# Score masks in 32-row matmuls, and a liquid state divided by DT * DT

## The chip, the cores and the metric

The kernel runs on one core of a Trainium2 chip. The metric is the time of one execution in device microseconds. The median of eight runs of the kernel before is 1016.46 us, the lowest 1014.69 us, the highest 1020.36 us. Engines are named as in the profile: PE is the tensor engine's matmul, PEld its weight load, DVE the vector engine, ACT the scalar engine, POOL the general-purpose engine, SP the engine that issues the DMAs. PSUM is the memory that matmuls write, in 8 banks of 128 partitions x 512 f32.

## The reference

One decoder block over x of 2 x 1024 tokens x 256 features. What matters here, in short:

```python
# self-attention on LN(LN(x)), 2*2 blocks of 512 tokens, 16 heads of 16; causal
scores = q @ k.T / sqrt(16);  scores[key > query] = -inf
attn = softmax(scores) @ v @ out_w + out_b
# liquid cell, 8 steps, DT = 0.1; ctx = attn, xs starts as LN(x + attn)*g1 + b1, vs as 0
u  = tanh(ctx @ w_ctx + xs @ w_x + b_inl)
vs = vs + DT * (u - xs - vs)
xs = xs + DT * vs
# then: x + xs, LN, GELU feed-forward of 1024, cross-attention to 77 context tokens (16 heads),
# and 8 soft trees of 255 nodes: (x @ W_in.T), silu, one path a tree kept, @ W_out.T
```

The kernel holds the 2 x 1024 tokens as four blocks of 512 (`NTB`), two to a sequence; the queries of a sequence's second block also attend to its first block, whole and without a mask.

## The kernel before, in words

All work is issued by `Clock.weave` (L354). Several threads of stages, written as Python generators, run beside each other: attention scores of blocks 0 and 2, of blocks 1 and 3, weights, the middle (liquid cell, feed-forward, cross-attention) and the trees. A stage yields what it needs next (tiles, banks, or a ready operation), and `weave` takes the one that its own costs say can start first. These costs are written into `Clock`: a change of the PE array's shape (`TURNS`, L100), a matmul, an eviction. So one changed cost moves the order of everything behind it. The order is fixed when the program is built; on the chip each engine works its queue in that order and waits on semaphores.

PE works in three shapes. FULL is 128 rows x 128 columns. ROWS is four groups of 32 rows x 128 columns that work beside each other: a group holds 4 heads, 32 partitions each, and each head is one group of rows. COLUMNS is four groups of 128 x 32, for the products of weights and values.

Causal attention is worked in sets of heads (`Heads`, L71). There are two kinds. `maxima` (L797) writes the scores of one tile of queries with q as the weights and keys as columns, and DVE reads each bank for the maximum. `weighted` (L874) writes transposed scores, and ACT reads each bank for the exponential; POOL clears what lies above the diagonal. A unit has four heads, one PSUM bank each, and `Clock.issue` (L310) writes either all four heads of one unit, or two heads of one and two of a unit of the other engine ("mixed"), or two alone. `Clock.choices` (L278) picks: the price of a mixed pair holds half of the difference of the two spans.

In the block on the diagonal, `maxima` has three units for each of 4 groups and 4 blocks: queries' tiles 0 and 2 together (128 and 384 keys in one bank), tile 1 (256 keys) and tile 3 (512 keys). Their last 128 keys need the causal mask. `masks` (L815) adds it ahead of the scores, one bf16 matmul of the 128 x 128 identity with the 128 x 128 mask for every head and tile, in shape FULL; the scores then follow in shape ROWS onto the same banks. `issue` writes the masks of all heads first (L315-317), then the scores step by step.

`liquid` (L965) keeps two banks of pre-activations for a block. Each of 8 steps takes ACT's tanh into `w`, one DVE add of `r` (or a subtraction of `xs` in the first step), eight matmul instructions with `w_dx` (which is `w_x` times DT * DT, made in `fill_late`, L561), and then on DVE for each half `xs = w * DT*DT + xs` and `r = w * (1 - DT) - xs`. The product ahead of the first step uses `w_x` itself. In the end `add_tokens_first` (L637) transposes `xs` and adds it to `h0` with `add_half` (L652).

`fill` (L548) prepares memory at the start: it clears tiles, and copies mask and identity to bf16.

Of the kernel before, what the change touches and what calls it, by code (L numbers as in the profile page):

```python
# [16 lines left out]
P = 128  # L17
# [53 lines left out]
class Heads:  # L71
# [4 lines left out]

    def __init__(self, banks, columns, one, read, engine, mask=None):
        self.banks, self.one, self.read, self.engine = banks, one, read, engine
        self.mask, self.steps = mask, len(columns)
        self.mode = FULL if mask else ROWS  # L80
        self.span = sum(max(n, P) for n in columns) / 600
        self.left = [0, 2] if engine == "dve" else [2, 0]
        self.over = 0
# [8 lines left out]
class Clock:  # L92
# [185 lines left out]
    def choices(self, t, todo):  # L278
# [15 lines left out]
        one = max(self.pe, ready, free[1][0]) + self.ALONE  # L294
        found.append((one, self.turn(own.mode), [(own, own.left[0])]))
        if len(own.left) == 2:
            found.append((two, self.turn(own.mode), [(own, 0), (own, 2)]))
        for u in todo:
            other = None if isinstance(u["need"], (Op, list)) else u["need"][1]
            if not isinstance(other, Heads) or other.engine == own.engine:  # L300
                continue
            at = max(two, self.ready(u["need"][0]) + self.HANDOVER)
            for j0 in own.left:
                if 2 - j0 in other.left:
                    worth = self.turn(max(own.mode, other.mode)) - self.MIXED
                    worth += abs(own.span - other.span) / 2
                    found.append((at, worth, [(own, j0), (other, 2 - j0)]))
        return found

    def issue(self, heads):  # L310


        heads = [(unit, j0 + i) for unit, j0 in heads for i in range(2)]
        heads = [(unit, j, *unit.banks(1)) for unit, j in heads]
        for unit, j, ps in heads:  # L315
            if unit.mask:
                unit.mask(j, ps)
        self.each = max(unit.span for unit, _, _ in heads) / sum(unit.steps for unit, _, _ in heads)
        for step in range(max(unit.steps for unit, _, _ in heads)):

            for unit, j, ps in reversed(heads):
                if step < unit.steps:
                    unit.one(j, ps, step)
        pairs = []
        for (unit, j0, one), (_, j1, two) in zip(heads[::2], heads[1::2]):
            unit.left.remove(j0)
            pairs.append((unit, self.reading(unit, (unit.read(j0, one), one), (unit.read(j1, two), two))))
        return pairs
# [86 lines left out]
def decoder_kernel(ctx: ExitStack, tc: tile.TileContext, ins: dict, out: bass.AP):  # L415
# [80 lines left out]
    wo = load("wo", (DC, D))  # L496
    w_x = load("w_x", (DC, D))
    xwq = load("xwq", (DC, D))
# [13 lines left out]
    make_causal_mask(nc, mask32, NEG)  # L512
    mask, ident16 = (const.tile([P, P], BF16, tag=n, name=n) for n in ("mask", "ident16"))
    half = const.tile([P, NQ], F32, tag="half", name="half")
# [3 lines left out]
    paths = const.tile([P, 2, P], BF16, tag="paths16", name="paths16")  # L518
    w_dx = const.tile([P, DC, D], F32, tag="w_dx", name="w_dx")
    half_b = const.tile([P, 2 * PAR], F32, tag="half_b", name="half_b")  # L520

# [26 lines left out]
    def fill():  # L548
# [4 lines left out]
        )  # L553
        yield clock.vector("tensor_copy", mask, mask32)
        yield clock.vector("tensor_copy", ident16, ident)
        for t in (v, *xv):
# [4 lines left out]
    def fill_late():  # L561
        for t in (qT[1], xq, *nmax[2:]):
            yield zeros(t)
        yield clock.vector("tensor_copy", paths, paths32)
        yield clock.activation(w_dx, w_x, AF.Copy, scale=DT * DT)
        for name in ("ff", "trees"):
            for w in streams[name]:
# [43 lines left out]
    def scaled(dst, src, mv, rstd):  # L611

        for i in range(NQ):
# [3 lines left out]
            )  # L617

    def evicted(ops, *banks):
        yield ops  # L620
        clock.free(*banks)

    def features_first(dst, src, name, g=None, b=None):

        made = []
        for c in range(DC):
            yield (src,), 1
            ps = bank()
            for i in range(NQ):
                clock.transpose(  # L630
                    ps[:, i * P : (i + 1) * P], src[:, i, c * P : (c + 1) * P], ident
                )
            affine = () if g is None else (col(g, c), col(b, c))
            made.append(clock.beside(evicted(clock.evict(dst[:, c, :], ps, *affine), ps)))
        yield (), lambda: all(m() for m in made)

    def add_tokens_first(dst, src, name):  # L637

        made = []
        for j in range(2):  # L640
            yield (src,), 1
            ps = bank()
            for i in range(2):
                for c in range(DC):
# [3 lines left out]
                    )  # L648
            made.append(clock.beside(add_half(dst, j, ps)))
        yield (), lambda: all(m() for m in made)  # L650

    def add_half(dst, j, ps):  # L652

        at = dst[:, 2 * j : 2 * j + 2, :]
        yield clock.vector("tensor_tensor", at, at, ps.rearrange("p (i d) -> p i d", d=D), ALU.add)
        clock.free(ps)
# [98 lines left out]
    def norms(tb, x):  # L755
# [6 lines left out]
        xn = atile(f"xn{tb}", "xn", 2)  # L762
        yield from features_first(xn, xc, f"attn{tb}", "g_attn", "b_attn")
        return xn
# [32 lines left out]
    def maxima(tb, g, qT):  # L797
# [14 lines left out]
        for parts in units:  # L812
            diagonal = parts[0][1] == blk

            def masks(j, ps):  # L815
                for _, _, n, at in parts:
                    clock.matmul(
                        ps[:, at + n - P : at + n], ident16, mask, start=at == 0, stop=False,
                        skip_group_check=True,
                    )  # L820

# [20 lines left out]
            k = parts[0][1] * TB  # L842
            heads = Heads(banks, columns, one, read, "dve", masks if diagonal else None)
            yield (qT[:, g, :], kT[:, g, k : k + TB]), heads
# [100 lines left out]

    def layernorm(src, name, g=None, b=None, known=None):

# [4 lines left out]
        dst = dtile(f"xn_{name}")  # L952
        yield from features_first(dst, xc, name, g, b)
        return dst
# [10 lines left out]
    def liquid(tb, h0, aT):  # L965
# [8 lines left out]
        done.add((tb, "o"))  # L974
        xs = yield from layernorm(h0, f"l1_{tb}", "g1", "b1", block[tb]["known"])
        yield from add_product(ps, w_x, xs)
        r = dtile(f"r{tb}")
        for it in range(NITER):


# [3 lines left out]
            for c in range(DC):  # L984
                if it == 0:
                    yield clock.vector("tensor_tensor", w[:, c, :], w[:, c, :], xs[:, c, :], ALU.subtract)
                else:
                    yield clock.vector("tensor_tensor", w[:, c, :], w[:, c, :], r[:, c, :], ALU.add)
            if it < NITER - 1:
                yield from add_product(ps, w_dx, w)  # L990
            for c in range(DC):
                yield clock.vector("scalar_tensor_tensor", 
                    xs[:, c, :], w[:, c, :], DT * DT, xs[:, c, :], ALU.mult, ALU.add
                )
                if it < NITER - 1:
                    yield clock.vector("scalar_tensor_tensor", 
                        r[:, c, :], w[:, c, :], 1.0 - DT, xs[:, c, :], ALU.mult, ALU.subtract
                    )
        clock.free(*ps)
        yield from add_tokens_first(h0, xs, f"xs{tb}")  # L1000

# [11 lines left out]
    def feed_forward(tb, x, h0):  # L1013
        hn = yield from layernorm(h0, f"l2_{tb}", "g2", "b2")
        yield clock.vector("tensor_tensor", x, x, h0, ALU.add)
# [390 lines left out]
```

## Time and profile before

| what | value |
| --- | --- |
| median of 8 runs | 1016.46 us |
| profiled execution | 1016.75 us, its span 1015.0 us, so 1.7 us lie around the span |
| granted PE clock over the span | 0.988 |
| POOL, DMA | busy 82.2 us; 44.87 MB moved, mean 44 GB/s |
| masks | 256 matmuls of 128 x 128 bf16 |
| scores, DVE's kind / ACT's kind | 768 / 768 matmul passes |
| liquid cell | 224 matmul passes, 184 large DVE operations |

A record of a matmul lasts longer than the array is taken: it runs from its issue to the write of its last result. An f32 matmul is two passes, and each is a record. "Busy" of a group is the union of its records. A timeline line merges records of one kind that follow each other: its first number is the start, its second the time from that start to the last record's end.

### The profile page before, as it was taken

The page shows a single profiled execution, that of the slowest core. Times are in us where ns is not written, and L with a number is a line of the kernel's source. Part 1 is how long each engine was busy: PE and PEld are TensorE (multiplying, and loading weights), DVE is VectorE, ACT ScalarE, POOL GpSimd, SP SyncE. Part 2 cuts the span into 40 slices and gives each one's busy share as a digit, 9 for nine tenths or more (in the row PEclk, how much of TensorE's full clock was granted, in tenths as well). Part 3 has the DMA queues.
Part 4 walks back from the last instruction along what each step waited for, and adds up shares of the span by engine and source line. Part 5 has one row for each costly group of instructions (what it writes and reads, how often), then busy time and mean ns, then how long its engine had stood idle before and what let it go on. Part 6 is the DMA issues. An engine that isn't in the chain of part 4 may idle for free.

```text
span 1015.0 us, 14070 instructions
## 1 busy us (share of the span) xinstructions
PE 964.7 (95%) x5496; PEld 486.0 (48%) x5496; DVE 620.9 (61%) x1345; ACT 412.5 (41%) x695; POOL 82.2 (8%) x161
## 2 busy tenths in 40 slices
PE   6899899899999999999999999999999999999898
PEld 4544444345446445564444433346455446645443
DVE  4757768953544798608766996841465881555444
ACT  4153344533473234415444444542643423353331
POOL 0111101010101002102100101010100000000000
PEclk9799999999999999999999999999999999999999
DMA  8220001002000001123000001102200021101211
GB/s 286 63 46 19 1 1 42 1 21 84 22 2 21 32 10 44 31 73 94 22 11 12 12 21 42 43 13 88 67 12 32 31 84 52 44 30 58 83 63 57
DMA packets 22338, 44.87 MB, mean 44 GB/s; under 512 B 2944, under 2 KB 3328, under 8 KB 22272
## 3 DMA queue, kind: packets, MB, share of 16 engines
q1 hardware_dynamic: 22272, 43.97, 13.8%
q8 instruction: 43, 0.70, 0.3%
q14 instruction: 23, 0.19, 0.1%
HBM read 35.57 MB, written 2.10 MB: 37 GB/s over the span
## 4 chain that ended last, share of the span: by engine, by line
PE 87%; DVE 7%; ACT 4%; DMA 1%; issue 1%; SPq 0%; ACTq 0%; DVEq 0%
PE bank L165 81%; PE bank L181 6%; ACT p L197 2%; DVE nmax L207 2%; DVE top L207 2%; DVE ta L207 1%; DMA xwk_sb<-in_xwk_dram 1%; ACT xp L197 0%; ACT th L197 0%; DMA xn<-in_xtok_dram 0%; DVE xn_l L207 0%; DVE x L207 0%; ACT ta L197 0%; DVE r L207 0%; DVE xc_l L207 0%
## 5 line engine op out<-in xcount | busy, mean ns | idle before, releaser
L197 ACT ACTIVATE p<-bank 128x512 f32<-128x512 f32 (+1 forms) x320 | 155.4, 556 | 153.3 <-PE bank L165 143.6
L207 DVE TENSOR_REDUCE top<-bank 128x1 f32<-128x512 f32 (+3 forms) x256 | 138.1, 583 | 47.1 <-PE bank L165 46.8
L165 PE MATMUL bank<-qT,kT 32*128 32x512 f32 (+3 forms) x768 | 131.4, 534 | 7.8 <-ACT p L197 3.4
L165 PE MATMUL bank<-kT,qT 32*128 32x512 f32 (+3 forms) x768 | 131.9, 543 | 6.8 <-ACT p L197 4.0
L165 PE MATMUL bank<-ta,trees 128*128 128x512 f32 x256 | 126.2, 601 | 2.7 <-DVE ta L207 2.5
L165 PE MATMUL bank<-xn_t,trees 128*128 128x512 f32 x256 | 126.6, 604 | 0.4 <-ACT p L197 0.2
L207 DVE TENSOR_REDUCE nmax<-bank 128x4 f32<-128x308 f32 (+4 forms) x192 | 83.5, 479 | 39.5 <-PE bank L165 37.0
L165 PE MATMUL bank<-w,w_dx 128*128 128x512 f32 x224 | 102.7, 598 | 1.4 <-DVE w L207 1.4
L207 DVE TENSOR_TENSOR x<-x,bank 128x512 f32<-128x512 f32 x40 | 27.3, 685 | 115.3 <-PE bank L165 115.1
L216 POOL TENSOR_SCALAR_AFFINE_SELECT p<-p 128x256 f32<-128x256 f32 x128 | 56.5, 463 | 400.9 <-ACT p L197 226.4
L197 ACT ACTIVATE th<-bank,half_b 128x512 f32<-128x512 f32 x64 | 44.1, 689 | 100.6 <-PE bank L165 100.6
L197 ACT ACTIVATE w<-bank,b_ac 128x512 f32<-128x512 f32 x64 | 43.9, 688 | 86.9 <-PE bank L165 86.8
L165 PE MATMUL bank<-p,v 128*32 128x512 f32 (+3 forms) x768 | 72.3, 500 | 1.4 <-DVE nmax L207 1.0
L165 PEld LDWEIGHTS bank<-ta,trees 128*128 128x128 f32 x256 | 46.2, 190 | 52.9 <-issue 42.9
L165 PEld LDWEIGHTS bank<-xn_t,trees 128*128 128x128 f32 x256 | 44.7, 190 | 51.6 <-issue 43.0
L165 PEld LDWEIGHTS bank<-qT,kT 32*128 32x128 f32 x768 | 48.1, 188 | 40.6 <-ACT p L197 13.3
L165 PEld LDWEIGHTS bank<-w,w_dx 128*128 128x128 f32 x224 | 41.3, 190 | 53.4 <-issue 41.2
L165 PEld LDWEIGHTS bank<-kT,qT 32*128 32x128 f32 x768 | 43.6, 189 | 48.4 <-ACT p L197 11.6
L165 PE MATMUL bank<-xn_l,ff 128*128 128x512 f32 x128 | 59.7, 594 | 0.0
L165 PE MATMUL bank<-ff,ht 128*128 128x256 f32 x256 | 59.2, 379 | 0.0
L207 DVE SCALAR_TENSOR_TENSOR ta<-ta,th 128x1024 f32<-128x1024 f32 x32 | 39.1, 1222 | 30.2 <-ACT ta L197 30.1
L165 PEld LDWEIGHTS bank<-ff,ht 128*128 128x128 f32 x256 | 48.6, 190 | 16.9 <-issue 11.5
(168 smaller groups left out, 1165.1 us busy)
## 6 DMA issues: line engine op xcount, KB each, us to landing
trees<-in_trees_dram SPq DMA_DIRECT2D x64, 256.0 KB, 2.6
ff<-in_ff_dram SPq DMA_DIRECT2D x32, 256.0 KB, 3.0
xn<-in_xtok_dram SPq DMA_DIRECT2D x4, 512.0 KB, 4.1
qT<-qc SPq DMA_DIRECT2D x16, 128.0 KB, 2.3
kT<-kc SPq DMA_DIRECT2D x16, 128.0 KB, 2.3
kc<-in_xtok_dram SPq DMA_DIRECT2D x4, 512.0 KB, 4.4
x<-in_xtok_dram SPq DMA_DIRECT2D x4, 512.0 KB, 4.0
xq<-xqc SPq DMA_DIRECT2D x16, 128.0 KB, 2.3
```

Source lines behind the costliest of these rows:

```text
L165: return self.nc.tensor.matmul(out, w, x, **kw)
L181: return self.nc.tensor.transpose(out, x, ident)
L197: lambda: self.nc.scalar.activation(out, x, func, bias=bias, scale=scale),
L207: "dve", cost, 0.085, out, args, lambda: getattr(self.nc.vector, name)(out, *args, **kw)
L216: self.nc.gpsimd.affine_select(out=out, in_=args[0], **kw)
```

## The change

- Masks. `mask` and `ident16` become tiles of 4 x 128 columns in which every group of 32 rows holds one 32-row slice after another, so that the four heads' groups of rows can each add the mask by themselves. A mask of one head and tile is now four bf16 matmuls in shape ROWS (32 rows each), over the last 128, 96, 64 and 32 columns, since the first 32 rows of the mask touch all columns and later ones fewer. `issue` runs them as the first steps of a head, interleaved over the heads like the scores. A unit's span counts 0.056 us for each mask step, and no unit asks for shape FULL any more.
- Making those tiles: `fill` copies mask and identity to bf16, spreads the identity over `rows`, and multiplies eight times 128 x 128 on PE into two banks, which are copied out.
- Liquid cell. The state is `z = xs / (DT*DT)`: scale and bias of its LayerNorm are divided by DT * DT into `g1b1` once. The first product uses `w_dx` as the others do. The add after tanh becomes `w = r * DT*DT + w`; `r` is worked out from the old `z`; the state's update becomes the plain sum `z = z + w`, which is issued beside the rest and only has to be done before the next `r`. `add_half` multiplies by DT * DT when it adds the state to `h0`.
- `w_x` is loaded into one of the trees' buffers, since it is used only to make `w_dx`.

```diff
-    def __init__(self, banks, columns, one, read, engine, mask=None):
+    def __init__(self, banks, columns, one, read, engine, mask=None, masks=0):
...
-        self.mode = FULL if mask else ROWS
-        self.span = sum(max(n, P) for n in columns) / 600
+        self.span = sum(max(n, P) for n in columns) / 600 + masks * 0.056
...
-        found.append((one, self.turn(own.mode), [(own, own.left[0])]))
+        found.append((one, self.turn(ROWS), [(own, own.left[0])]))
...
-                    worth = self.turn(max(own.mode, other.mode)) - self.MIXED
+                    worth = self.turn(ROWS) - self.MIXED
                     worth += abs(own.span - other.span) / 2
...
-        for unit, j, ps in heads:
-            if unit.mask:
-                unit.mask(j, ps)
-        self.each = max(unit.span for unit, _, _ in heads) / sum(unit.steps for unit, _, _ in heads)
-        for step in range(max(unit.steps for unit, _, _ in heads)):
+        n = sum(unit.masks + unit.steps for unit, _, _ in heads)
+        self.each = max(unit.span for unit, _, _ in heads) / n
+        for step in range(max(unit.masks + unit.steps for unit, _, _ in heads)):
             for unit, j, ps in reversed(heads):
-                if step < unit.steps:
-                    unit.one(j, ps, step)
+                if step < unit.masks:
+                    unit.mask(j, ps, step)
+                elif step < unit.masks + unit.steps:
+                    unit.one(j, ps, step - unit.masks)
...
-    w_x = load("w_x", (DC, D))
+    w_x = load("w_x", (DC, D), pool=work, tag="tree", bufs=5)
...
-        yield clock.vector("tensor_copy", mask, mask32)
-        yield clock.vector("tensor_copy", ident16, ident)
+        yield clock.vector("tensor_copy", both[:, 0, :], mask32)
+        yield clock.vector("tensor_copy", both[:, 1, :], ident)
+        rows_of = both[:, 1, :].rearrange("p (r o k) -> p r o k", o=1, k=SLOT)
+        yield clock.vector(
+            "tensor_copy", rows.rearrange("p r (j k) -> p r j k", k=SLOT),
+            rows_of.to_broadcast([P, 4, 4, SLOT]),
+        )
+        for i, dst in enumerate((mask, ident16)):
+            yield (both, rows), 1
+            ps = bank()
+            for r in range(4):
+                clock.matmul(
+                    ps[:, r * P : (r + 1) * P], rows[:, r, :], both[:, i, :], start=True, stop=True
+                )
+            yield clock.evict(dst.rearrange("p r k -> p (r k)"), ps)
+            clock.free(ps)
...
+        yield clock.vector(
+            "tensor_scalar", g1b1, vecs[:, at : at + 2 * DC], 1.0 / (DT * DT), None, ALU.mult
+        )
...
-        yield clock.vector("tensor_tensor", at, at, ps.rearrange("p (i d) -> p i d", d=D), ALU.add)
+        if scale is None:
+            yield clock.vector("tensor_tensor", at, at, two, ALU.add)
+        else:
+            yield clock.vector("scalar_tensor_tensor", at, two, scale, at, ALU.mult, ALU.add)
...
-            def masks(j, ps):
-                for _, _, n, at in parts:
-                    clock.matmul(
-                        ps[:, at + n - P : at + n], ident16, mask, start=at == 0, stop=False,
-                        skip_group_check=True,
-                    )
+            def masks(j, ps, i):
+                _, _, n, at = parts[i // 4]
+                r, i = slice(j * SLOT, (j + 1) * SLOT), i % 4
+                keys = slice(i * SLOT, P)
+                clock.matmul(
+                    ps[:, at + n - P + i * SLOT : at + n], ident16[r, i, :], mask[r, i, keys],
+                    start=at == i == 0, stop=False, skip_group_check=True,
+                )
...
-        yield from add_product(ps, w_x, xs)
-        r = dtile(f"r{tb}")
+        yield from add_product(ps, w_dx, z)
+        r, kept = dtile(f"r{tb}"), []
...
-                if it == 0:
-                    yield clock.vector("tensor_tensor", w[:, c, :], w[:, c, :], xs[:, c, :], ALU.subtract)
-                else:
-                    yield clock.vector("tensor_tensor", w[:, c, :], w[:, c, :], r[:, c, :], ALU.add)
+                yield clock.vector(
+                    "scalar_tensor_tensor", w[:, c, :], (r if it else z)[:, c, :],
+                    DT * DT if it else -DT * DT, w[:, c, :], ALU.mult, ALU.add,
+                )
             if it < NITER - 1:
                 yield from add_product(ps, w_dx, w)
+            yield (), lambda: all(k() for k in kept)
             for c in range(DC):
-                yield clock.vector("scalar_tensor_tensor", 
-                    xs[:, c, :], w[:, c, :], DT * DT, xs[:, c, :], ALU.mult, ALU.add
-                )
                 if it < NITER - 1:
-                    yield clock.vector("scalar_tensor_tensor", 
-                        r[:, c, :], w[:, c, :], 1.0 - DT, xs[:, c, :], ALU.mult, ALU.subtract
-                    )
+                    yield clock.vector(
+                        "scalar_tensor_tensor", r[:, c, :], w[:, c, :],
+                        (1.0 - DT - DT * DT) / (DT * DT), z[:, c, :], ALU.mult, ALU.subtract,
+                    )
+            for c in range(DC):
+                args = "tensor_tensor", z[:, c, :], z[:, c, :], w[:, c, :], ALU.add
+                kept.append(clock.beside(once(clock.vector(*args))))
```

Left out: `once`, a generator of one operation; `features_first` and `layernorm` take a list of scale and bias columns in place of two names.

## The prediction

> **What bounds the kernel now.** I read the busy shares first, then the chain, then PE's groups by shape, and then stretches of the timeline that show what one set of heads costs.
>
> ```profile
> PE 964.7 (95%) x5496; PEld 486.0 (48%) x5496; DVE 620.9 (61%) x1345; ACT 412.5 (41%) x695; POOL 82.2 (8%) x161
> PE 87%; DVE 7%; ACT 4%; DMA 1%; issue 1%; SPq 0%; ACTq 0%; DVEq 0%
> ```
>
> PE is the bound: 95% busy and 87% of the chain. No other engine is near. So the change is worth what it takes off PE's array, less what turns into waits for DVE and ACT.
>
> ```profile
> L165 PE MATMUL bank<-w,w_dx 128*128 128x512 f32 x224 | 102.7, 598 | 1.4 <-DVE w L207 1.4
> L165 PE MATMUL bank<-mask,ident 128*128 128x128 bf16 x256 | 29.3, 224 | 7.0 <-ACT p L197 5.3 <-DVE nmax L207 0.7 <-DVE top L207 0.7
> L165 PE MATMUL bank<-xk,xq 32*128 32x77 f32 x512 | 26.6, 277 | 1.8 <-DVE nmax L207 0.8 <-ACT p L197 0.6 <-ACT th L197 0.3
> ```
>
> These are PE's groups by shape. The masks' 29.3 us holds each record's tail, so it is not what they take. That comes from the timeline:
>
> ```profile
> 147.56 3.60 PE L165 MATMUL bank<-w,w_dx 128*128 128x512 f32 x8
> ...
> 64.03 0.39 PE L165 MATMUL bank<-mask,ident 128*128 128x128 bf16 x4
> 64.35 0.71 PE L165 MATMUL bank<-kT,qT 32*128 32x256 f32 x8
> 64.97 1.14 PE L165 MATMUL bank<-qT,kT 32*128 32x512 f32 x8
> 66.04 0.70 PE L165 MATMUL bank<-xn,wk_sb 128*128 128x512 f32 x1
> ```
>
> ```profile
> 64.34 0.31 PEld L165 LDWEIGHTS bank<-kT,qT 32*128 32x128 f32 x8
> ```
>
> ```profile
> 270.92 1.13 PE L165 MATMUL bank<-xk,xq 32*128 32x77 f32 x32 [0.64 <-ACT p L197]
> ```
>
> ```profile
> L165 PE MATMUL bank<-w,w_dx x224: 592/592/697, 147.6 to 821.8; 128*128 128x512 f32 x112
> ```
>
> Five prices follow.
> - Pass and tail. Eight passes take 3.60 us and one lasts 0.592: (3.60 - 0.592)/7 = 0.430 us from start to start, so a record has a tail of about 162 ns. One of the 224 passes lasts 697: after a change of shape the first f32 load of 128 columns is in the open, 105 ns.
> - A mask in FULL: (390 - 219)/3 = 57 ns, 219 being the median record; I use 56.
> - A change of shape: the masks' last record ends at 64.42 and ROWS starts at 64.35, 70 ns inside the tail, so it costs 162 - 70 = 92 ns. The way out of ROWS, 66.11 to 66.04, is the same.
> - Groups of 32 rows load and run beside each other: eight loads begin and end within 0.31 us, though one lasts 181 ns.
> - 32 passes of 77 columns in four groups take (1130 - 270)/31 = 28 ns each, 111 ns for a step of four: the costliest short step in ROWS that the trace has.
>
> **Masks: what goes, comes and moves.** The order of instructions is fixed at build, so shapes can be counted in both kernels' orders.
>
> Changes of shape: 372 before, 300 after. A mask block stood in FULL between 67 sets and their scores; after, 50 sets carry masks, and they stay in ROWS. 72 x 92 = 6.6 us saved.
>
> First loads in the open: entries into ROWS with an f32 load go from 158 to 99 (31 more enter with a mask's bf16 load), f32 entries into FULL from 79 to 61; COLUMNS and transposes hardly move. (59 + 18) x 105 = 8.1 us saved. Against this, in 50 sets the scores' first load now stands behind a short mask matmul that covers 56 of its 105 ns: 50 x 49 = 2.5 us.
>
> The masks themselves: 256 x 56 = 14.3 us go. After, 46 sets of four heads of one unit and 4 sets of two have 16 x 8 + 30 x 4 + 4 x 4 = 264 steps. The trace has no bf16 matmul of 32 rows. Its bounds: 27 ns a step, if narrow steps shrink to the four issues seen at a set's start (8 loads and matmuls within some 27 ns); 111 ns, the 77-column row above. I take 56 ns, the FULL mask of the same type and at most the same columns, since in f32 the 32-row load costs at a change what the full one does. 264 x 56 = 14.8 us, 0.5 more than before.
>
> Sum at 56 ns: -6.6 - 8.1 + 2.5 + 0.5 = **-11.7 us** of array time. If steps follow their columns (56, 43, 29, 27, mean 39): 264 x 39 = 10.3 and 50 x 78 = 3.9 in the open, so -14.7 + 3.9 - 4.0 = -14.8. At 111 ns: 264 x 111 = 29.3, so -14.7 + 2.5 + 15.0 = +2.8.
>
> A rule speaks against the change. The Trainium skill, "TensorE: Matmul & The Clock Gate", section "Wait — 56ns, not 53.3ns?", says that matmuls never start closer than about 25 ns however few columns they have. The row of 77 columns (28 ns) agrees with it, the starts within a set's first four do not. By that rule a step of four costs an estimated 100 ns, and the sum would be about zero instead of -11.7. The same page, section "The mechanism", has neighbours in different row groups start about 4 ns apart, which is the case here; no run shows it yet for such short matmuls in a row.
>
> How much of 11.7 us reaches the end? For the 67 mask sets I set the timeline from the masks to the next FULL work against the sum of these prices: 41 agree within 0.15 us, so PE was the bound there, and 26 hold a wait for a reader of a bank. I count the first in full and half of the others: (41 + 13)/67 = 0.81, so -9.4 us.
>
> **What the masks move.** Before, 36 of the 67 sets were mixed pairs. After, none is: the counted mask steps put the pair's price above that of four heads of one unit. Sets that ACT alone reads go from 48 to 68, those that DVE alone reads and that carry masks from 29 to 46. ACT then has four banks of 0.6 us to clear from a set that takes PE about 1 us, DVE four of 0.68. What hides this is the dense work of the other threads. Without that cover, by the waits of now: PE waited 14.2 us for ACT's `p` beside 48 such sets, 0.30 each, and 11.8 us for DVE's `top` and `nmax` beside 49 sets, 0.24 each: 20 x 0.30 + 17 x 0.24 = +10 us. I take 0, as the stretches from 410 to 850 us hold hardly any PE wait, and keep +10 as the end.
>
> **Start.** DVE gets three bf16 copies in place of two and two copies out of PSUM ahead of the first statistics; PE gets eight matmuls there. Bounds: 0.2 to 0.8 us for the spread, 2 x 0.69 for the copies out, about 1 us for the matmuls and their waits: statistics up to 2.5 us late. The cover: `xc` is ready at 10.5 us and its transposes start at 13.55, behind weights that land by 12.65. Cost 0; without cover 2.5.
>
> **Liquid cell.** Per block and half, DVE had a plain add, two scalar_tensor_tensor; it has the same three in other places. Rows: TENSOR_TENSOR 689 ns, SCALAR_TENSOR_TENSOR 699 and 696. The add after tanh becomes the slower kind, 32 steps x 10 = 0.3 us on the way to the products; covered by trees and scores, else 0.3. `r` ended at 150.37 for an add that ran at 151.06, so it was not late before; it comes earlier now and frees nothing. Eight adds to `h0` become scalar_tensor_tensor reading PSUM: 746 against 684, 0.5 us of DVE at 61%. The scaling of `g1b1` is one operation of some 0.2 us on DVE at the start. `w_x` in a tree's buffer is read by 20 us, long before the trees. DMAs and POOL keep count and kind (SP 178, POOL 166). Together 0, bounds 0 to +1.
>
> **Clock.**
>
> ```profile
> 0.00:52.00 52.00, 39.60 (x211) 25.18 (x212) 31.58 (x101) 16.27 (x18) 6.13 (x14) 0.87 0.52 170
> ```
>
> In the first 52 us PE had 0.87 of its clock (the last three columns are clock, DMA share, GB/s): 7 us lost around the first sets. The new order may move this by some us either way; I take 0.
>
> **Sum.** The profiled execution took 1016.75 us (span 1015.0 and 1.7 around it), 0.3 above the median. 1016.5 - 9.4 = **1007 us**.
>
> **The rivals.**
> - A, the forecast: steps of about 56 ns, four fifths kept. For it: equal f32 loads in both shapes. 1007 us, own range 1003 to 1011.
> - B, steps shrink with their columns and all of it is kept: -14.8, so 1002 us. For it: PE's 87% of the chain. Against: the 26 waiting sets.
> - C, the waits take it: sets with one reader hold their banks longer. -9.4 + 10 gives 1017, half of the waits 1012; I put it at 1014. For it: the 0.24 to 0.30 us a set. Against: dense work beside it.
> - D, slower: short 32-row steps are bound by issue or load as in the 77-column row, at 111 ns. +2.8 us, 1019 us. It decides from (14.7 - 2.5 + 14.3)/264 = 100 ns a step on; below, the change gains. For it: that row is the only sustained short ROWS work. Against: its f32 loads take 105 ns by themselves.
> - That the liquid cell's edit does anything by itself I put at under 1 us either way, within A to D.
>
> **How the numbers follow.** A 0.43, B 0.15, C 0.22, D 0.20. A difference under 0.2% (2 us) is about what a measurement of this kernel can't tell from none. Faster: all of A and B, 0.6 of C, little of D: 0.72. Within: 0.3 of C and of D: 0.12. Slower: 0.16. The range takes B's end and most of D: 1000 to 1020, with the clock's few us inside it.
>
> **What would show it.** Right: mask steps start about 40 to 60 ns apart in each group, PE's busy time falls by some 10 us, the waits for `p` and `top` stay near 26 us. D: steps 100 ns or more apart. C: PE busy down by 10, idle up by as much. Wrong altogether: a new order that leaves PE without dense work at the start or end, or a clock cut elsewhere than in the first 52 us.

## The result: slower, though the array got its work off

The changed kernel takes **1020.31 us** (median of 21 runs, 1017.63 to 1024.03). The kernel before took 1015.79 us beside it (median of 62, 1012.09 to 1020.48). The ratio is **1.0046** with an interval of [1.0035, 1.0058]: 0.46% slower, some 4.7 us. Forecast were 1007 us, and 1020 as the upper end of the range.

| | before | after |
| --- | --- | --- |
| profiled execution, span | 1015.0 us | 1015.7 us |
| PE busy | 964.7 | 945.8 |
| span less PE busy | 50.3 | 69.9 |
| array, counted | 919.4 | 903.6 |
| span less array ("waits") | 95.7 | 112.1 |

The profiled execution of after, 1017.4 us with the 1.7 around its span, is 2.9 us below the median of that kernel, so the two spans show less of the loss than the medians do. The two lower rows are a count: I went through each kernel's matmuls in their order and gave each its price from the trace of before (the prediction's five prices; mask steps by their columns). Between changes of shape the count agrees with the trace of before within 0.1 us in 256 stretches of 372; what lies above it is called waiting, and holds the time lost in stretches in which the trace shows PE granted half its clock.

Busy shares of after, then three of PE's groups by shape and the mask steps by their columns:

```profile
PE 945.8 (93%) x6272; PEld 475.6 (47%) x6272; DVE 621.3 (61%) x1355; ACT 407.6 (40%) x689; POOL 82.7 (8%) x161
```

```profile
L164 PE MATMUL bank<-w,w_dx 128*128 128x512 f32 x224 | 102.2, 599 | 4.0 <-DVE w L206 3.8
L164 PE MATMUL bank<-xk,xq 32*128 32x77 f32 x512 | 24.5, 277 | 4.3 <-ACT p L196 2.4 <-ACT xp L196 1.3 <-DVE xq L206 0.4
```

```profile
L164 PE MATMUL bank<-mask,ident 32*128 32x128 bf16 x256 | 15.1, 224 | 11.6 <-ACT p L196 6.3 <-ACT xp L196 1.7 <-DVE at L206 1.6
L164 PE MATMUL bank<-mask,ident 32*128 32x96 bf16 x256 | 13.9, 208 | 0.0
L164 PE MATMUL bank<-mask,ident 32*128 32x64 bf16 x256 | 13.2, 193 | 0.0
L164 PE MATMUL bank<-mask,ident 32*128 32x32 bf16 x256 | 12.4, 178 | 0.0
```

PE's busy time fell by 18.9 us and the time in which it is not busy rose by 19.6. The records of mask steps get shorter by 15 to 16 ns for every 32 columns less (224, 208, 193, 178 ns), which tells of the columns, not yet of the distance from step to step. That is seen in the timeline of after (start, time to the last record's end):

```profile
99.71 0.33 PE L164 MATMUL bank<-mask,ident 32*128 32x128 bf16 x16 [1.23 <-ACT p L196]
99.87 0.70 PE L164 MATMUL bank<-kT,qT 32*128 32x256 f32 x8
100.38 1.24 PE L164 MATMUL bank<-qT,kT 32*128 32x384 f32 x10
```

Sixteen mask matmuls, four steps in four groups of rows, are over in 0.33 us with the last record's tail, and the scores start 0.16 us after the first mask: 40 ns a step. Over the 41 whole sets of the trace that begin at full clock, a group's next start comes on average 62, 42, 28 and 29 ns behind a step of 128, 96, 64 and 32 columns (behind the first mostly 55 or 66), 40 ns over all. So steps follow their columns down to 64, and one of 32 takes no less. The four groups of one step start 4 ns apart in the median, 5.0 on average.

The array got what the prediction asked of it, and a little more. The time went into waits. PE's waits, by what it waited for (total us, times, longest), before and then after:

```profile
PE bank L165 <- ACT p L197: 14.2, 27, 1.4
PE bank L165 <- DMA w_ctx_sb<-in_w_ctx_dram: 7.7, 1, 7.7
PE bank L165 <- DVE top L207: 6.2, 11, 1.4
PE bank L165 <- DVE w L207: 1.4, 2, 0.8
PE bank L165 <- ACT xp L197: 0.7, 1, 0.7
```

```profile
PE bank L164 <- ACT p L196: 21.5, 29, 1.7
PE bank L164 <- DVE top L206: 7.9, 11, 1.4
PE bank L164 <- DVE rows L206: 4.7, 1, 4.7
PE bank L164 <- ACT xp L196: 4.6, 8, 1.2
PE bank L180 <- DVE xn_l L206: 4.1, 1, 4.1
PE bank L164 <- DVE w L206: 3.8, 5, 1.3
```

No single wait carries the loss: `p` +7.3, `xp` +3.9 (cross-attention's exponentials), `w` +2.4, `top` +1.7, one wait of 4.1 for `xn_l`. The 4.7 for `rows`, the making of the masks, stands against 6.1 less for the first weights. But most of it stands in one place, ahead of self-attention scores. The scores of 512 columns, before and then after (the number behind the second bar is PE's idle time just before the group):

```profile
L165 PE MATMUL bank<-kT,qT 32*128 32x512 f32 x384 | 91.4, 659 | 6.8 <-ACT p L197 4.0 <-DVE top L207 2.7
L165 PE MATMUL bank<-qT,kT 32*128 32x512 f32 x384 | 90.9, 648 | 4.4 <-ACT p L197 2.0 <-DVE top L207 0.9 <-ACT th L197 0.8
```

```profile
L164 PE MATMUL bank<-kT,qT 32*128 32x512 f32 x384 | 81.7, 657 | 11.3 <-ACT p L196 6.3 <-DVE top L206 3.9 <-DVE nmax L206 1.0
L164 PE MATMUL bank<-qT,kT 32*128 32x512 f32 x384 | 77.2, 653 | 8.5 <-ACT p L196 3.3 <-DVE top L206 1.9 <-ACT xp L196 1.5
```

With the masks (7.0 and 11.6) and the shorter scores, the idle time ahead of self-attention scores and their masks sums up to 21.6 us before and 36.5 after: 14.9 of the 19.6. Most of the waits for `xp` (3.3 of 4.6) stand there too, ahead of masks and scores and not of cross-attention's own. Where in the span it happens is seen in stretches (busy us of PE, PEld, DVE, ACT, POOL with counts; then granted clock, DMA share, GB/s), before and after:

```profile
0.00:150.00 150.00, 129.58 (x906) 69.63 (x907) 97.14 (x256) 55.47 (x95) 20.46 (x48) 0.94 0.22 70
150.00:300.00 150.00, 138.44 (x939) 65.96 (x937) 92.62 (x194) 69.87 (x127) 13.21 (x25) 0.98 0.10 29
650.00:950.00 300.00, 295.25 (x1472) 154.06 (x1471) 158.47 (x329) 119.17 (x191) 13.98 (x23) 1.00 0.15 47
```

```profile
0.00:150.00 150.00, 125.15 (x1149) 67.96 (x1150) 100.99 (x258) 58.12 (x100) 19.47 (x48) 0.97 0.25 78
150.00:300.00 150.00, 129.18 (x1084) 62.31 (x1087) 91.23 (x201) 64.11 (x119) 13.38 (x25) 0.95 0.07 22
650.00:950.00 300.00, 293.66 (x1575) 151.67 (x1568) 160.85 (x340) 118.59 (x194) 13.30 (x23) 1.00 0.14 45
```

From 150 to 300 us PE is busy 129.2 us in place of 138.4. By the count, the waits grew by 0.7 us up to 150, by 10.2 between 150 and 300, and by 5.4 behind 300; by time in which PE is not busy, 4.4, 9.3 and 5.9. The two differ because half clock counts as waiting: up to 150 us before spent 17.1 us at half clock and after 10.2, between 150 and 300 it is 6.8 and 13.7 us, each worth at most half of its length. The trees, long dense matmuls, begin at 326 us in both kernels. So by either reading two thirds of the loss lie where the prediction's cover doesn't exist yet. One place of it, the end of the first block's liquid cell, before and after:

```profile
188.88 1.92 PE L165 MATMUL bank<-p,v 128*32 128x512 f32 x16
189.71 1.29 DVE L207 SCALAR_TENSOR_TENSOR xn_l<-w,xn_l 128x512 f32<-128x512 f32 x2
190.74 0.70 PE L165 MATMUL bank<-kT,qT 32*128 32x512 f32 x2
191.81 1.09 PE L181 MATMUL bank<-ident,xn_l 128*128 128x128 f32 x8
```

```profile
173.19 1.88 DVE L206 TENSOR_REDUCE top<-bank 128x1 f32<-128x512 f32 x3
174.98 1.29 DVE L206 SCALAR_TENSOR_TENSOR r<-w,xn_l 128x512 f32<-128x512 f32 x2
176.18 1.29 DVE L206 SCALAR_TENSOR_TENSOR w<-r,w 128x512 f32<-128x512 f32 x2
177.38 2.50 DVE L206 TENSOR_TENSOR xn_l<-xn_l,w 128x512 f32<-128x512 f32 x4
179.34 1.93 PE L180 MATMUL bank<-ident,xn_l 128*128 128x128 f32 x6 [4.12 <-DVE xn_l L206]
```

Before, scores and values of other blocks ran on PE while DVE finished the state (`xn_l`); the transposes came without a wait. After, no such work stood there: three reads of `top` stood ahead of `r`, four sums, two of them put off from the step before, stood at the end, and PE stood for 4.12 us.

### The profile page after: what moved, and what is told of

Same layout as the page of the kernel before. It is cut to its first block, busy times and chain, and to the rows that moved or that the text cites. A ratio compares the mean times of both kernels' runs of the same rounds, so it can differ in the third digit from the quotient of the medians.

```text
span 1015.7 us, 15615 instructions
## 1 busy us (share of the span) xinstructions
PE 945.8 (93%) x6272; PEld 475.6 (47%) x6272; DVE 621.3 (61%) x1355; ACT 407.6 (40%) x689; POOL 82.7 (8%) x161
## 4 chain that ended last, share of the span: by engine, by line
PE 52%; DVE 2%; ACT 2%; issue 1%; DMA 0%; DVEq 0%; ACTq 0%
PE bank L164 49%; PE bank L180 3%; ACT p L196 1%; DVE ta L206 1%; ACT xp L196 1%; DVE nmax L206 0%; DVE top L206 0%; DMA trees<-in_trees_dram 0%; DVE w L206 0%; DVE x L206 0%; DVE xc_x L206 0%; ACT th L196 0%; DVE xn_l L206 0%; DVE r L206 0%; DVE h L206 0%
## 5 line engine op out<-in xcount | busy, mean ns | idle before, releaser
L196 ACT ACTIVATE p<-bank 128x512 f32<-128x512 f32 (+1 forms) x320 | 153.3, 558 | 134.2 <-PE bank L164 131.4
L164 PE MATMUL bank<-ta,trees 128*128 128x512 f32 x256 | 123.3, 598 | 1.6 <-DMA trees<-in_trees_dram 1.0
L164 PE MATMUL bank<-qT,kT 32*128 32x512 f32 (+3 forms) x768 | 111.1, 535 | 13.6 <-ACT p L196 6.0
L164 PE MATMUL bank<-kT,qT 32*128 32x512 f32 (+3 forms) x768 | 113.0, 544 | 11.3 <-ACT p L196 6.3
L206 DVE TENSOR_REDUCE nmax<-bank 128x1 f32<-128x128 f32 (+3 forms) x192 | 82.6, 478 | 36.2 <-PE bank L164 36.2
L164 PEld LDWEIGHTS bank<-qT,kT 32*128 32x128 f32 x768 | 41.8, 189 | 54.0 <-ACT p L196 19.0
L164 PEld LDWEIGHTS bank<-kT,qT 32*128 32x128 f32 x768 | 38.7, 196 | 44.9 <-ACT p L196 17.9
```

The lines of the kernel that those rows point to most:

```text
L164: return self.nc.tensor.matmul(out, w, x, **kw)
L196: lambda: self.nc.scalar.activation(out, x, func, bias=bias, scale=scale),
L206: "dve", cost, 0.085, out, args, lambda: getattr(self.nc.vector, name)(out, *args, **kw)
```

## The experiments

The theory after this: the operations gain, and the new order, which the planner makes from the changed costs, loses more. Rivals: the put-off sum of the state alone (SUM), the sets with one reader alone (READERS), the pace of the trees, or the liquid cell by itself.

### One part at a time, planned anew

**e1_liquid_only**: the kernel before with the changed liquid cell; masks as before.

```diff
-        yield from add_product(ps, w_x, xs)
+        yield from add_product(ps, w_dx, z)
...
```

> The changed liquid cell with the masks of before (128-row matmuls, mixed pairs). Before 1015.8 us, changed 1020.3. Theory READERS (mask sets with one reader make PE wait): the liquid edit is innocent, so 1014 to 1018 us. Theory SUM (the sum of z, put off behind r, stands ahead of the closing transposes and of the next r): slower than before, 1018 to 1022. Theory ORDER (any new order moves the end by some us, no single cause): anywhere in 1010 to 1021.

Measured: 1048.08 us, ratio 1.0308 [1.0268, 1.0348]. An edit that leaves DVE almost the same operations costs 3%, more than any of the three theories had. The count gives 918.2 us of array, like before, and 129.4 of waits.

**e2_sum_in_place**: the changed kernel with the sum back in its old place, ahead of `r`.

```diff
-            yield (), lambda: all(k() for k in kept)
             for c in range(DC):
+                yield clock.vector("tensor_tensor", z[:, c, :], z[:, c, :], w[:, c, :], ALU.add)
...
-                kept.append(clock.beside(once(clock.vector(*args))))
...
```

> The changed kernel with z = z + w back in its old place, ahead of r in each half, waited for as before; masks in 32-row matmuls as in the change. SUM: the 4 us hole of PE at the end of the first block's liquid cell goes, 1006 to 1013 us. READERS: no better than the change, 1018 to 1022 us. ORDER: 1010 to 1021.

Measured: 1021.5 us, 1.007 [1.0044, 1.0096]. SUM falls: without the put-off sums it is no faster, and PE still stands 3.8 us for `xn_l`, 3.5 of them at once, so the stand at the end of the liquid cell needs no put-off sum.

**e3_mixed_pairs**: the changed kernel, the price of a pair worked out without the mask steps, so that pairs of both engines come back.

```diff
-                    worth += abs(own.span - other.span) / 2
+                    worth += abs(own.plain - other.plain) / 2
```

> The changed kernel, but the price of a mixed pair compares the two spans without the mask steps, so that mask sets may again be pairs of one DVE unit and one ACT unit. READERS: PE's idle time falls from 70 towards 50 us and the array time of some 904 us shows: 1003 to 1010 us. SUM: the waits stay, 1017 to 1022 us. ORDER: 1008 to 1021.

Measured: 1043.66 us, 1.0274 [1.0242, 1.0306]. PE's waits for `p` in its trace, against 14.2 before and 21.5 after:

```profile
PE bank L165 <- ACT p L197: 28.9, 41, 1.2
```

No theory had a time like this one. With the pairs back the waits for `p` grow, which speaks against READERS; but the whole order is another again, so it doesn't rule it out.

**e4_before_shifted**: the kernel before with a slightly other order, one cost of the planner changed.

```diff
-    HANDOVER = 0.06
+    HANDOVER = 0.07
```

> The kernel before with one planning constant changed (the hand-over between engines counted as 0.07 us in place of 0.06): the same operations on each engine, in another order; PE's array time is 0.4 us longer by count. READERS and SUM: 1014 to 1018 us, as before. ORDER: it differs from before by 3 us or more either way.

Measured: 1016.09 us, 1.0012 [0.9996, 1.0029]: this nudge costs the kernel before at most 0.3%. ORDER had expected 3 us or more either way, so not every new order costs time.

### The same order with other operations

These take the planner out. Each decision of `weave` and each bank that it took is written down as a list and played back (`place_in` is the thread, `pairs` the heads):

```diff
-        while todo:
-            best = None
...
+        for place_in, which, pairs in chosen:
+            now = todo[place_in]
+            heads = [(todo[i]["need"][1], j0) for i, j0 in pairs]
...
-        got = [i for _, i in self.free_banks()[:n]]
+        got = [next(self.took) for _ in range(n)]
```

**o1_change_on_before**: all changed operations in the order of before (the sum directly behind `r`). **o2_masks_on_before**: the same with the sum ahead of `r`. **o3_liquid_on_before**: the changed liquid cell alone, in the order of before. **o4_fullmasks_on_after**: the order of after with the masks of before (one matmul of 128 rows); the liquid cell stays changed.

> All operations of the change (32-row masks, liquid cell with r first and then the plain sum), but issued in the order of the kernel before, turn by turn and bank by bank, written down as a list; mixed pairs stay where they were, the mask tiles are made at the start ahead of the rest. Array time by count 913 against 919 us: 36 changes of shape fewer. Theory ORDER (the operations gain, the new order loses): faster than before by 3 to 6 us, 1009 to 1013. Theory OPERATIONS (short matmuls or the new liquid steps cost more than their count): no faster than before, 1015 to 1022.

> As the run with all of the change in the order of before, but the sum of z stays ahead of r as before. ORDER: the same time within 2 us, 1009 to 1013. OPERATIONS by the liquid cell: clearly faster than the run with r first; by the masks: 1015 to 1022.

> The 128-row masks of before with the liquid cell's new operations (r first, then the sum) in the order of before. The same edit with its own order took 1048 us. ORDER: 1013 to 1017, no different from before. OPERATIONS by the liquid cell: well above, 1025 to 1048.

> The order of the changed kernel, its liquid cell and its start, but every mask set writes its masks as 128-row matmuls again (47 changes of shape more, array time by count 914 against 904 us). ORDER: the changed kernel's 1020 and most of these 11 us, 1026 to 1032. OPERATIONS by the masks: no slower than the change, 1014 to 1021.

| | order of before | order of after |
| --- | --- | --- |
| masks of 128 rows | 1 (o3: 0.9997 [0.9979, 1.0015]) | o4: 1.0071 [1.0048, 1.0093] |
| masks of 32 rows | o1: 0.9963 [0.9943, 0.9982], o2: 0.9964 [0.9944, 0.9984] | 1.0046 [1.0035, 1.0058] |

The medians are 1012.58 (o1), 1012.89 (o2), 1016.9 (o3) and 1024.51 us (o4), beside 1016.46 for before. Read by column, the masks gain: 0.37% in the old order, clear of noise, and 0.25% in the new, at the edge of what the intervals can tell. Read by row, the new order loses 0.7 to 0.8%, about 8 us, whichever masks it carries. The liquid cell's operations cost nothing that can be told from noise (0.15% at most). o1 and o2 are the fastest versions tried, and beat both kernels. o1 to o3 lie where ORDER had them; o4 lies between both theories (1026 to 1032, 1014 to 1021): of the 10.8 us of array time that short masks save in the new order only some 2.5 to 4 arrive. The idle time ahead of self-attention scores and masks, summed as above, goes the same way: 21.6 us before, 24.3 in o1, 30.3 in o4, 36.5 in after. With the same operations the new order adds 12.2 us there (o1 to after).

In the order of before the count gives the changed operations 913.2 us, 6.2 less than before, not 15.8: changes of shape go from 372 to 336, not to 300. The other 9.6 us of the counted gain come with the new order, and so do the waits.

In o3's trace the group of the liquid cell's products is what it was before (102.7 us, 598 ns, 1.4 us of waits):

```profile
L165 PE MATMUL bank<-w,w_dx 128*128 128x512 f32 x224 | 102.6, 598 | 1.4 <-DVE w L207 1.4
```

### The planner nudged

Does any order that is planned for the changed operations do as well? The nudges are `HANDOVER` 0.07 (as in e4), `MARGIN` (a constant in the planner's price of a stage whose data are not ready yet) 0.8 in place of 0.7, and later due times of the trees:

```diff
-        [(EACH * (n + 1) + 110, EACH * (n + 2) + 110, 62, 0.2, leaves(n)) for n in range(NTB)],
+        [(EACH * (n + 1) + 150, EACH * (n + 2) + 150, 62, 0.2, leaves(n)) for n in range(NTB)],
```

(180 in p4.) p1 is e1, and p2 and p4 are e3, with a nudge; p3, s3 and s4 are the changed kernel; s1 and s2 the kernel before.

> The liquid cell alone (1048 us with its own order), planned with a hand-over of 0.07 us in place of 0.06. Counted along PE's order in array time, block 0's trees now end at 572 us, as block 1's begin, in place of 465, before block 1's cross-attention at 499. Theory PACE (the loss is trees, the only dense work, spent before the serial chain of the middle needs cover): back to 1013 to 1019 us. Theory CLASH (the new liquid steps and mixed pairs get in each other's way): 1040 or more.

> The changed kernel with mixed pairs allowed again (1044 us with its own order), planned with a hand-over of 0.07 us. Array time by count 903 us; block 0's trees end at 542 where block 1's begin at 543, block 3's cross-attention comes at 815 in place of 840. PACE: 998 to 1008 us, faster than before. CLASH: 1035 or more.

> The changed kernel with the trees' due times 40 us later. Array time by count 903 us as in the change; block 0's trees end at 535 in place of 520, block 3's cross-attention comes at 815 in place of 832. PACE: some of the change's waits behind 450 us go, 1010 to 1017 us. If the change's loss is all in its first 300 us, where there are no trees (10.8 of its 16.4 us of added waits): no faster than 1015.

> The changed kernel with mixed pairs allowed and the trees' due times 70 us later; array time by count 902 us, block 0's trees end at 558, block 3's cross-attention at 814. PACE: 998 to 1008 us. CLASH: 1035 or more.

> The kernel before planned with MARGIN 0.8 in place of 0.7: same operations, another order, array time 918 us by count, trees paced as before (block 0's end at 555 where block 1's begin at 558). DRAW (the old order of 1016 is the good one among many that its constants were set for; a changed plan gets an ordinary one): 1018 to 1030. SYSTEMATIC (the planner makes good orders of the old kernel and worse ones of the changed one): 1014 to 1019.

> The kernel before with the trees' due times 40 us later, as was done to the changed kernel (1028). By count 916 us of array time; block 0's trees end at 461, before block 1's cross-attention at 500, as in the two orders that took 1044 and 1048. DRAW and PACE: 1035 to 1050. SYSTEMATIC: 1014 to 1022.

> The changed kernel planned with a hand-over of 0.07 us, as was done to the kernel before (1016). Array time 906 us by count. DRAW: anywhere in 1008 to 1035. SYSTEMATIC: 1019 to 1030, above every order of the kernel before with the same setting.

> The changed kernel planned with MARGIN 0.8; array time 907 us by count. DRAW: anywhere in 1008 to 1035. SYSTEMATIC: 1019 to 1030, above the kernel before with MARGIN 0.8.

| planner | before | liquid cell alone | the change | the change with pairs |
| --- | --- | --- | --- | --- |
| as it is | 1 | e1 1.0308 | 1.0046 | e3 1.0274 |
| HANDOVER 0.07 | e4 1.0012 | p1 1.0085 [1.0054, 1.0115] | s3 1.0217 [1.0178, 1.0256] | p2 1.0142 [1.0106, 1.0177] |
| MARGIN 0.8 | s1 1.0019 [1.0002, 1.0036] | | s4 1.021 [1.0168, 1.0251] | |
| trees later | s2 1.0169 [1.013, 1.0209] | | p3 1.0114 [1.0085, 1.0142] | p4 1.016 [1.012, 1.02] |

Later trees take 1.1% off e3, and a nudge of 0.01 takes 2.2% off e1, so these two were unlucky orders, but no order that is planned from start to end gets down to the 0.9963 that the same operations reach in the order of before. The order of before is not robust either: with later trees it is 1.7% slower. The small nudges leave it alone and cost the change 1.6 to 1.7% more. The order that the change came with is the best of its orders tried. PACE fell: p1 (1024.55 us), p2 (1030.85), p3 (1028.16) and p4 (1035.03) all lie above its ranges, and p3 is slower than the change; CLASH's ranges are met by p4 alone. Between DRAW and SYSTEMATIC nothing is settled: s1 (1016.02) fits SYSTEMATIC alone, s2 (1031.42) lies between the two, s3 (1035.73) and s4 (1036.28) lie above both, by about 1 us for DRAW.

Four of the slow orders (e1, e3, s4 and the h2 below; 1036 to 1048 us) share one line in the waits near the end, which neither before nor after has. In e1:

```profile
PE bank L181 <- DVE xc_t L207: 4.8, 1, 4.8
```

There the last block comes to the statistics ahead of its trees when nothing is left to run beside it. s3 and p4, as slow as some of these (1036 and 1035 us), do not have it. So slow orders have no single cause, and I did not find one quantity that ranks them.

### The old beginning, planned anew behind it

**h1_old_to_326**: the changed operations follow the list up to the first matmul of the trees; from there the planner decides with the changed costs, and the sums of blocks 1 to 3 are put off as in the change. **h2_old_to_130**: the list ends ahead of the first liquid cell.

```diff
+        while todo:
+            if chosen:
+                place_in, which, pairs = chosen.pop(0)
+                now = todo[place_in]
...
+            else:
+                best = None
+                for t in todo:
```

> The changed operations follow the order of the kernel before up to the first matmul of the trees (326 us in both traces), and from there the planner decides with the changed costs, as in the changed kernel. By a count with the trace's prices the array then holds 908.7 us of work, against 913.2 with the old order throughout and 903.6 in the changed kernel. Theory START: the new order loses its time before the trees begin, where little dense work stands beside the sets (+10.8 of the +16.4 us of waits lay in the first 300 us). Then the old beginning takes that away: 1008 to 1014 us. Theory ALONG: the new order loses it wherever unmixed sets stand, or by the trees' pace behind 326 us: then 1018 to 1030 us. Between 1014 and 1018 it would be some of both.

> As the run with the old order up to the trees, but the old order ends at about 128 us, ahead of the first block's liquid cell; the planner decides from there with the changed costs. The array holds 906.4 us by the count with the trace's prices. Theory FIRST SETS: the new order loses its time in the first 130 us, in the sets of block 0 with masks. Then this kernel keeps what the old beginning gave: 1012 to 1017 us. Theory LIQUID: it loses it between 130 and 326 us, where the first block's liquid cell, feed-forward and cross-attention run beside the sets of the other blocks and no tree is there. Then the time is that of the changed kernel or more: 1019 to 1030 us. A value of 1017 to 1019 tells nothing.

h1: 1015.86 us beside 1016.91, ratio 0.9981 [0.9955, 1.0008]. The median lies in the stretch that I had put down to "some of both". By the ratios, of the 0.83% between the two orders 0.65% goes with the beginning and 0.18% with the rest; the first lies clear of after's interval, the second can't be told from nothing. The stretches of h1's trace:

```profile
0.00:150.00 150.00, 127.33 (x1214) 68.78 (x1215) 100.71 (x264) 58.10 (x100) 20.35 (x48) 0.98 0.23 71
150.00:300.00 150.00, 138.34 (x1035) 65.15 (x1037) 89.97 (x191) 69.19 (x127) 13.22 (x25) 0.95 0.10 29
```

PE is busy 138.3 us from 150 to 300, as before, and the wait of 4.1 for `xn_l` is gone; the counted waits there are 25.8 us (23.0 before, 33.2 after). The granted clock is 0.95, as in after, so it is not the clock that separates these two (before has 0.98 there).

h2: 1036.24 us beside 1016.39, ratio 1.02 [1.0165, 1.0235], slower than I had expected of either theory. The old order up to 128 us alone doesn't save the new one; in that the result is on the side of LIQUID. But by the count its waits from 150 to 300 are 29.6 us, less than after's, and its loss lies elsewhere: 11.2 us from 550 to 650 (4.8 in after) and 30.1 behind 650 (18.9). So it doesn't show what LIQUID claims. The end, where PE stands after the last cross-attention product:

```profile
952.12 3.62 PE L165 MATMUL bank<-xwo_sb,xaT 128*128 128x256 f32 x16
960.51 2.30 PE L181 MATMUL bank<-ident,xc_t 128*128 128x128 f32 x8 [4.78 <-DVE xc_t L207]
```

The counted waits side by side, by the start of the stretch:

| | 0 to 150 | 150 to 300 | behind 300 | array | span |
| --- | --- | --- | --- | --- | --- |
| before | 38.2 | 23.0 | 34.6 | 919.4 | 1015.0 |
| after | 38.9 | 33.2 | 40.0 | 903.6 | 1015.7 |
| o4 | 39.4 | 29.0 | 39.7 | 914.4 | 1022.5 |
| o1 | 41.5 | 26.7 | 35.5 | 913.2 | 1016.9 |
| h1 | 38.9 | 25.8 | 41.2 | 908.7 | 1014.6 |
| h2 | 40.0 | 29.6 | 55.2 | 906.4 | 1031.1 |

Single executions differ by the half clock that they met: the profiled one of o1 is 6 us above its median, with 36 us of its span at half clock against 25 in before and 29 in after.

## Why the prediction was wrong, point by point

- **Bound by PE's array: right for the kernel before.** In its order a part of the saved array time arrived (o1). In the new order PE's busy time fell by 18.9 us and the span didn't.
- **Changes of shape, 372 to 300, first loads and the masks' own steps: right in kind, the step mis-sized.** I took 56 ns a step, the price of a full mask; measured are 62, 42, 28 and 29, mean 40, close to rival B's 39. The array went down by 15.8 us by the count where I had -11.7. D, 111 ns a step, is out. Its sum was also 2.5 us too high: a step of 111 ns would have covered the scores' first load of 105 ns, so it should have read +0.3.
- **The rule of 25 ns.** The Trainium skill, "TensorE: Matmul & The Clock Gate", "Wait — 56ns, not 53.3ns?", has starts never closer than about 25 ns, by which a step of four would take an estimated 100 ns. Steps took 28 to 62 ns, so across row groups the rule doesn't hold here; within one group no kind of step had its next start closer than 28 ns on average, which agrees. "The mechanism" of the same page has neighbours in different row groups about 4 ns apart; the trace of after shows 4 in the median.
- **Kept share 0.81: not contradicted.** In the same order 3.9 us of 6.2 counted arrived, 0.63; o1's interval, -1.8 to -5.8 us, allows 0.3 to 0.94. But the share was put on a sum that comes with another order, and there it means little.
- **"What the masks move", cost 0: this is the step that failed.** I priced the new order's waits at 0 with +10 as the end, "as the stretches from 410 to 850 us hold hardly any PE wait". The counted waits rose by 16.4 us. The order costs 0.7 to 0.8%, 7 to 8 us with the array time that it saves already taken off, with either kind of mask (o4, o1 and after). Two thirds of the rise lie ahead of 300 us, where no tree runs yet. The trace of before had this: trees start at 326.3, and 23 us of waits stood between 150 and 300 already. h1 agrees: with the old order up to the trees most of the loss is gone. That missing cover is the reason was not varied by itself.
- **Rival C: the outcome and the place; its reason is not shown.** The waits took it, and more than the price put on them: ahead of self-attention scores and masks the idle time rose by 14.9 us, where C's end was 10. That sets with one reader are the reason was only argued. With the pairs back PE stands there no less, 42.8 us in e3, 37.2 in p2 and 40.3 in p4 against 36.5 in after, though each of these has an order of its own. `w` and `xn_l` have no part in score sets, and rose by 6.5 us together.
- **Start, 0: right.** PE waits 4.7 us for `rows`, but its first work starts at 4.7 us in place of 7.7, and the transposes of `xc` at 12.91 in place of 13.55. The 4.4 us by which PE's idle time up to 150 us rose come behind that.
- **Liquid cell, 0 to +1 us: right as an operation** (o3, 0.9997). It was wrong as an edit to a planned kernel: let the planner order it anew, and it costs 3.1% (e1), or 0.85% with a nudge (p1).
- **Clock, 0: right within its few us.** Time at half clock is 29 us against 25, at most 2 us of waits in these two executions.

Open: which of the changed costs (the mask steps in a unit's span, the missing pairs, the sums that are put off, the shape of a unit) turns the planner to worse orders. e2 and e3 each take one back and don't mend it, but each also gets an order of its own.

## What to carry to other kernels

Where costs written into a planner decide the order, an edit is two edits: its operations, and a new order of everything behind it. Price the first by replaying the old order with the new operations; here that gave the gain (0.37%) that the edit as made turned into a loss (0.46%), and it is the version to keep. Price the second by where the saved time would have to be filled: here two thirds of the new waits lay ahead of 300 us, and the trees that were to cover them begin at 326.

## What was not expected

- Short 32-row bf16 matmuls in four row groups run at 28 to 62 ns a step of four, neighbours 4 ns apart in the median, each with its own weight load: a step of 28 ns has no room for a load like the first f32 one of 105 ns.
- An edit that leaves the operations and their durations almost as they were moved the time by 3.1% (e1), and a planner's cost moved by 0.01 us took 2.2% of it back (p1).
- PE's busy time was a poor guide: after has 18.9 us less of it than before in a span 0.7 us longer, and o1, the fastest by its median, shows 965.4 us, more than before, in an execution with 11 us more at half clock.
